# Which work stands in the turn of the loop before the first group of heads: one transformer block, two edits of the order and two extra warming products

## The chip, the cores and the metric

The kernel runs on one core of a Trainium2 chip. The metric is device time in microseconds (us), the median of three runs. The core has five engines that run side by side, each through its own list of instructions in order: TensorE (PE; its weight loads are shown apart as PEld), VectorE (DVE), ScalarE (ACT), GpSimd (POOL) and SyncE (SP, which here only issues DMA transfers). TensorE writes its results into PSUM, here eight banks of 128 x 512 float32; VectorE and ScalarE read them from there.

## The reference

The block modulates, attends and routes. With x of 8 rows x 512 tokens x 256 features and c of 8 x 256:

```
mod = (silu(c) @ wmod)                      # six vectors per row: sa, ca, ga, sb, cb, gb
h = layernorm(x) * (1 + ca) + sa
Q = h @ Wq.T ;  latent_k, latent_v = h @ Wk_down.T, h @ Wv_down.T      # 16 heads of 16, latent of 64
logits = (Q @ q_to_latent) @ latent_k.T / 8, causal
x = x + ga * (softmax(logits) @ latent_v @ v_up) @ Wout.T
h = layernorm(x) * (1 + cb) + sb
x = x + gb * (mixture of 16 experts on 512 chosen tokens each + a shared feed-forward)(h)
```

Everything is float32. Attention takes the first 570 us of the profiled execution; selection, experts and the rest of the shared feed-forward take the remainder. The change lies in the first 56 us.

## The kernel before, in words

**Set-up.** A tile `warm` of zeros is filled by VectorE, and five products of it with itself (lines 175 to 176) keep TensorE going while the inputs arrive. Each is 512 columns wide on the full 128 x 128 array; a float32 product is two instructions (two passes). Then VectorE forms the statistics of the first row's four token tiles, the first modulation `pmT` (line 207) is multiplied (16 passes of only 8 columns), VectorE takes it out of PSUM into `saT` and `caT` (lines 214 and 215), normalises the first row (`xn`), TensorE transposes it (`turn_h`, line 458), ScalarE applies the modulation, and TensorE multiplies the latents (line 468), the query (line 547) and the key (line 559) of the first group. Two row-wise modulation products per `modulate` (line 222) follow.

**Groups and turns.** The 16 heads of a row are worked on four at a time; such a group is a `Step`, n = 0 to 31, and four steps make a row. The loop runs n from -1 to 31. In turn n, the group n + 1 gets its row maxima: 16 products `scores` (line 569), each reduced by one VectorE instruction (`maxima`, line 575). At the same time the group n gets its transposed scores (`scores_t`, line 598) and ScalarE's exponentials (`exps`, line 609), after `fold` (lines 590 and 591) has turned the maxima into a column of the query, and the group n - 1 gets its products with the values (`context`, line 628). So turn -1 holds only the 16 maxima of group 0, and turn 0 holds the maxima of group 1 and the exponentials of group 0. Scores have a contraction of 32, so that each occupies a quarter of the array's rows, and their widths are 512, 384, 256 and 128 columns, four products of each.

**Query and key strips.** `query` multiplies 128 columns of Wq (two halves `c`, each two passes of 512 columns over all 128 rows); ScalarE copies the result (`spread`, line 537), and two DMAs on SP's queue (line 540) lay it out in the strips of two groups. Query and key of group 2 therefore serve groups 2 and 3 too, and are made in turn 0; group 2's scores come in turn 1.

**Order inside a turn.** `plan(n)` collects the other work of a turn as (earliest slot, estimated us, function). `laid_out` spreads it over nine slots: entries of 0.0 us go exactly where they are told; the others keep their order and are moved on, from their earliest slot, until a running budget `room` has space. `fill(k)` issues slot k: slot 0 before `fold`, slot k + 1 after the k-th pair of scores. Every engine then executes in the order in which it was issued. In turn 0 the plan holds the second modulation in transposed form (`modulate_t`, lines 225 to 240: 16 passes of 8 columns, each with its own 128 x 128 weight load, and two small VectorE instructions), four statistics of the next row, the query of group 2, its key with the first half of the values, and the second half of the values. Worked through `laid_out`, the modulation stands in slot 2, both halves of the query in slot 4, key and first values in slot 6, and the second values in slot 8.

**PSUM.** Tag "m" has two banks (`bank`), "s" and "t" three each (`bank_s`, `bank_t`). Scores of group 0 alternate between "s" and "t"; so TensorE can be six score products ahead of VectorE in turn -1, and three ahead later.

## Time and profile before

| what | value |
|---|---|
| median of three runs | 1443.43 us (1439.97 to 1443.79) |
| the profiled execution, its own time | 1438.41 us |
| its span | 1436.7 us |
| mean granted TensorE clock over the span | 0.97 |
| TensorE busy | 1379.9 us (96%) |
| VectorE busy | 906.9 us (63%) |
| start of turn 0 (first transpose of `fold`) | 31.96 us |
| start of turn 1 | 55.92 us |
| start of turn 2 | 69.53 us |

The profile divides the span into busy time per engine, a strip of 40 slices with the granted TensorE clock (`PEclk`, tenths of full speed), and groups of instructions by source line. A timeline row gives start, duration, engine, line, operation, output <- inputs, shapes and count, and in brackets the idle time of the engine before it with what ended that idle time. A table of stretches gives, for each stretch of the span, the busy time of each engine, the granted clock and the share of the DMA engines. "Busy" for TensorE means that a product is in flight, not that the array is full.

### The profile page before, as it was taken

How to read it: one execution, taken by the hardware profiler on the slowest of the kernel's cores; microseconds unless marked ns; L12 is line 12 of the kernel's file. 1: busy time of each engine (PE TensorE's matmuls, PEld its weight loads, DVE VectorE, ACT ScalarE, POOL GpSimd, SP SyncE). 2: the span in 40 equal slices, each digit the busy share in tenths (PEclk: the TensorE clock that was granted, in tenths of full speed). 3: DMA queues.
4: the chain of work that ended last, by engine and by line, in shares of the span. 5: the costliest groups of instructions: out<-in, count | busy, mean ns of one | idle time of the engine just before them, and what ended most of it. 6: DMA issues, size and time to landing. Idle time of an engine off the chain costs nothing. (4 is left out here: it accounts for less than half of the span.)

```text
span 1436.7 us, 21835 instructions
## 1 busy us (share of the span) xinstructions
PE 1379.9 (96%) x8010; PEld 932.0 (65%) x8010; DVE 906.9 (63%) x2383; ACT 475.9 (33%) x1100; POOL 561.7 (39%) x640
## 2 busy tenths in 40 slices
PE   8999999999999999997989999999999999999996
PEld 4545444444544445455555688888888888888885
DVE  4566666675666666335683477676677777776662
ACT  1455554555454553411001123232222223233221
POOL 4343524242524332402011555555444555555331
PEclk8899999999999999798999999999999999999998
DMA  7011111212121112025111434434544434434511
GB/s 235 23 28 30 46 30 41 32 41 39 49 36 41 31 42 48 22 39 206 34 35 48 128 105 134 127 86 135 137 124 116 135 102 132 133 85 130 137 16 15
DMA packets 75659, 113.28 MB, mean 79 GB/s; under 512 B 10136, under 2 KB 56856, under 8 KB 75552
## 3 DMA queue, kind: packets, MB, share of 16 engines
q1 hardware_dynamic: 60480, 85.40, 20.3%
q0 software_dynamic: 14336, 25.70, 9.3%
q8 instruction: 64, 1.05, 0.3%
q10 hardware_dynamic: 736, 0.79, 0.2%
q14 instruction: 43, 0.35, 0.1%
HBM read 86.40 MB, written 21.27 MB: 75 GB/s over the span
## 5 line engine op out<-in xcount | busy, mean ns | idle before, releaser
L575 DVE CUSTOM_DVE_ANT_0 sc_ps<-sc_ps,causal 128x256 f32<-128x256 f32 (+3 forms) x512 | 240.8, 514 | 123.2 <-PE st_ps L598 116.9
L609 ACT ACTIVATE p<-st_ps 128x256 f32<-128x256 f32 (+3 forms) x512 | 199.8, 438 | 254.9 <-PE st_ps L598 251.1
L569 PE MATMUL sc_ps<-k,q 32*128 32x512 f32 (+3 forms) x1024 | 253.1, 488 | 14.3 <-DVE mx L575 11.8
L598 PE MATMUL st_ps<-q,k 32*128 32x512 f32 (+3 forms) x1024 | 253.7, 491 | 1.5 <-ACT p L609 1.4
L613 POOL TENSOR_SCALAR_AFFINE_SELECT p<-p 128x256 f32<-128x256 f32 x256 | 104.7, 410 | 357.1 <-ACT p L609 356.4
L1114 PE MATMUL epy<-dw,emid 128*128 128x256 f32 x1024 | 236.0, 382 | 2.1 <-DVE emid L1085 1.1
L1137 POOL DMA_INDIRECT out<-eo,idx x64 | 102.6, 1602 | 318.7 <-DVE eo L1129 190.0
L1114 PEld LDWEIGHTS epy<-dw,emid 128*128 128x128 f32 x1024 | 192.0, 190 | 38.7 <-DVE emid L1085 13.2
L569 PEld LDWEIGHTS sc_ps<-k,q 32*128 32x128 f32 x1024 | 112.7, 189 | 133.4 <-DVE mx L575 80.6
L1062 ACT COPY c<-eu 128x256 f32<-128x256 f32 x120 | 44.7, 373 | 401.0 <-issue 227.5
L1045 PE MATMUL eu<-xsum,wsum 128*128 128x256 f32 x720 | 176.1, 381 | 0.0
L1045 PEld LDWEIGHTS eu<-xsum,wsum 128*128 128x128 f32 x720 | 135.7, 190 | 17.9
L1045 PE MATMUL eu<-xT,gu 128*128 128x256 f32 x480 | 142.8, 379 | 0.0
L598 PEld LDWEIGHTS st_ps<-q,k 32*128 32x128 f32 x1024 | 111.5, 190 | 7.6 <-ACT p L609 4.2
L1064 DVE TENSOR_TENSOR c<-eu,c 128x256 f32<-128x256 f32 x120 | 51.0, 425 | 100.9 <-ACT c L1063 98.5
L1085 DVE SCALAR_TENSOR_TENSOR emid<-eu,ub,esg 128x512 f32<-128x512 f32 x128 | 90.1, 743 | 30.6 <-ACT esg L1081 22.4
L1081 ACT ACTIVATE esg<-eu,gbias 128x512 f32<-128x512 f32 x128 | 81.5, 684 | 59.7 <-PE eu L1045 33.9
L1045 PEld LDWEIGHTS eu<-xT,gu 128*128 128x128 f32 x480 | 91.2, 190 | 12.4
L1065 DVE TENSOR_TENSOR eu<-eu,c 128x512 f32<-128x512 f32 x120 | 83.9, 699 | 4.1
L628 PE MATMUL po<-p,v 128*32 128x512 f32 (+3 forms) x1024 | 85.2, 452 | 0.5 <-DVE sg L297 0.4
L1002 POOL DMA_INDIRECT rows<-rows_d,idx x64 | 62.2, 972 | 40.1 <-DVE idx L995 18.4
L962 DVE TENSOR_TENSOR at_q<-pos_lo,iota 128x1024 bf16<-128x1024 f32 x64 | 75.2, 1217 | 0.0
(178 smaller groups left out, 1982.7 us busy)
## 6 DMA issues: line engine op xcount, KB each, us to landing
gu<-in_gw SPq DMA_DIRECT2D x16, 1024.0 KB, 4.9
gu<-in_up SPq DMA_DIRECT2D x16, 1024.0 KB, 7.1
dw<-in_dw SPq DMA_DIRECT2D x16, 1024.0 KB, 6.1
q<-q SPq DMA_DIRECT2D x32, 128.0 KB, 2.3
rows_d<-mod_d SPq DMA_DIRECT2D x8, 512.0 KB, 9.6
rows_d<-row SPq DMA_DIRECT2D x8, 512.0 KB, 3.0
out<-ysb SPq DMA_DIRECT2D x16, 256.0 KB, 2.1
k<-k SPq DMA_DIRECT2D x30, 128.0 KB, 2.3
```

The lines of the kernel that those rows point to most:

```text
L569: nc.tensor.matmul(sc_ps[:, 0:n], lhsT=self.q[k, i * P : (i + 1) * P], rhs=self.k[k, 0:n], start=True, stop=True)
L575: nc.vector.tensor_tensor_reduce(sc_ps[:, 0:n], sc_ps[:, 0:n], causal[:, T - n : T], 1.0, -3.0e38, ALU.add, ALU.max, self.m[:, i, o : o + 1],)
L598: nc.tensor.matmul(st_ps[:, 0:n], lhsT=self.k[k, c * P : (c + 1) * P], rhs=self.q[k, c * P : T], start=True, stop=True)
L609: nc.scalar.activation(self.p[c][:, j, :], st_ps[:, 0:n], AF.Exp, scale=SCALE)
L613: nc.gpsimd.affine_select(out=p, in_=p, pattern=[[0, 2], [1, P]], compare_op=ALU.is_ge, fill=0.0, base=0, channel_multiplier=-1,)
L628: nc.tensor.matmul(self.po[self.strip(j), c * P : T], lhsT=v[:, c, self.g * NG + j, :], rhs=self.p[c][:, j, :], start=(c == 0), stop=(c == ...
L1045: nc.tensor.matmul(self.u[:, q, :], lhsT=w, rhs=x, start=start, stop=True, skip_group_check=not start)
L1065: nc.vector.tensor_tensor(u[:, 1:3, :], u[:, 1:3, :], c3.unsqueeze(1).to_broadcast([P, 2, HC]), ALU.add)
L1081: nc.scalar.activation(sg, pg, AF.Silu, bias=gbias[:, e, f : f + 1])
L1085: nc.vector.scalar_tensor_tensor(mid[:, f, :], pu, ub[:, e, f : f + 1], sg, ALU.add, ALU.mult)
L1114: nc.tensor.matmul(self.py[:, jj, :], lhsT=self.mid[:, f, j * P : (j + 1) * P], rhs=self.dw[:, f, :], start=(n == 0), stop=(n == NF - 1),)
L1137: nc.gpsimd.indirect_dma_start(out=out[:, :], out_offset=bass.IndirectOffsetOnAxis(ap=t.idx[:, j : j + 1], axis=0), in_=eo[:, jj, :], in_o ...
```

## The change

Four edits. One more warming product of 512 columns (six in place of five) ahead of the statistics. One warming product of 256 columns after the first modulation. `modulate_t` and both halves of group 2's query leave the plan of turn 0 and enter that of turn -1, which was empty. The second half of the first row's values gets an earliest slot of 4 in place of 1 in turn 0.

Worked through `laid_out`, turn -1 then has the modulation in slot 4 (after eight of the 16 scores), the query's first half in slot 6 (after 12) and its second half in slot 8 (after all 16, ahead of `fold`). In turn 0, the key with the first values stands in slot 4, and the second values in slot 7; with an earliest slot of 1 for the latter, they would be in slot 7 as well.

```diff
-    for _ in range(5):
-        nc.tensor.matmul(bank_s("warm"), lhsT=warm[:, 0:P], rhs=warm, start=True, stop=True)
+
+    def keep_warm(n):
+        nc.tensor.matmul(bank_s("warm")[:, 0:n], lhsT=warm[:, 0:P], rhs=warm[:, 0:n], start=True, stop=True)
+
+    for _ in range(6):
+        keep_warm(T)
...
+    keep_warm(T // 2)
     nc.vector.tensor_copy(saT, pmT[:, 0:KC, :])
     nc.vector.tensor_scalar_add(caT, pmT[:, KC : 2 * KC, :], 1.0)
...
         if n < 0:
+            add(1, 1.8, modulate_t)
+            for c in range(KC):
+                add(2 + 2 * c, 0.86, lambda c=c: steps[2].query([c]))
             return todo
         if n == 0:
-            add(1, 1.8, modulate_t)
             for i in range(TT):
                 add(i, 0.0, lambda i=i: stats(TT + i, mv))
...
             for c in range(KC):
-                add(0, 0.86, lambda c=c: steps[n + 2].query([c]))
+                if n > 0:
+                    add(0, 0.86, lambda c=c: steps[n + 2].query([c]))
             if g > 0:
                 add(0, 0.9, steps[n + 2].key)
             else:
                 add(1, 1.8, lambda: (steps[n + 2].key(), rows[b].value(0)))
-                add(1, 0.9, lambda: rows[b].value(1))
+                add(1 if n > 0 else 4, 0.9, lambda: rows[b].value(1))
```

## The prediction

> **What bounds the kernel now.** I read the page first: TensorE is busy for 96% of the span, and its clock, full nearly everywhere, is lower in the first two slices.

> ```profile
> span 1436.7 us, 21835 instructions
> PE 1379.9 (96%) x8010; PEld 932.0 (65%) x8010; DVE 906.9 (63%) x2383; ACT 475.9 (33%) x1100; POOL 561.7 (39%) x640
> PEclk8899999999999999798999999999999999999998
> ```

> So I asked for the table of stretches over the first 54 us, cut where the clock changes (busy us with counts for each engine, then the clock, DMA share, GB/s).

> ```profile
> 9.26:12.67 3.41, 2.52 (x18) 2.14 (x18) 3.11 (x13) 0.00 (x0) 2.99 (x8) 1.00 1.01 345
> 12.67:16.08 3.41, 3.39 (x9) 1.95 (x9) 0.39 (x2) 1.55 (x2) 2.80 (x10) 0.50 0.02 8
> ...
> 26.32:29.74 3.42, 3.39 (x15) 1.80 (x13) 3.42 (x15) 0.00 (x0) 0.00 (x0) 1.00 1.10 350
> 29.74:33.15 3.41, 2.44 (x11) 1.74 (x9) 2.67 (x18) 0.00 (x0) 0.00 (x0) 0.50 1.11 345
> 33.15:36.56 3.41, 3.41 (x12) 1.88 (x14) 1.97 (x4) 0.54 (x2) 0.00 (x0) 0.50 1.06 371
> 36.56:39.98 3.42, 3.42 (x14) 1.81 (x9) 2.59 (x10) 1.74 (x4) 0.81 (x2) 0.50 0.07 19
> 39.98:43.39 3.41, 3.41 (x19) 3.04 (x21) 0.26 (x2) 0.00 (x0) 0.00 (x0) 0.50 0.00 0
> 43.39:46.80 3.41, 3.41 (x13) 1.34 (x8) 2.69 (x10) 1.85 (x4) 0.41 (x1) 0.50 0.00 0
> 46.80:50.22 3.42, 3.42 (x8) 1.06 (x10) 0.05 (x1) 0.28 (x1) 0.41 (x1) 0.50 0.00 0
> 50.22:53.63 3.41, 3.26 (x34) 1.96 (x30) 1.90 (x10) 2.19 (x7) 1.77 (x3) 1.00 0.36 77
> ```

> From 29.74 to 50.22 us the array runs at half clock, through nearly the whole of turn 0. The same table by turns, and the timeline around the two moved pieces:

> ```profile
> 31.96:55.92 23.96, 23.54 (x99) 13.20 (x99) 10.99 (x44) 7.97 (x20) 4.41 (x10) 0.62 0.31 93
> 55.92:69.53 13.61, 12.88 (x113) 6.91 (x113) 9.12 (x35) 7.69 (x20) 7.61 (x12) 1.00 0.02 5
> ```

> ```profile
> 38.67 3.58 PE L232 MATMUL pmT<-sc,wmod 128*128 128x8 f32 x16
> 46.13 3.78 PE L547 MATMUL pq<-hT,wq 128*128 128x512 f32 x4
> ```

> ```profile
> 42.29 0.17 DVE L239 COPY sbT<-pmT 128x16 f32<-128x16 f32 x1 [2.66 <-PE pmT L232]
> 50.74 0.43 DVE L575 CUSTOM_DVE_ANT_0 sc_ps<-sc_ps,causal 128x256 f32<-128x256 f32 x1 [3.89 <-PE st_ps L598]
> ```

> Turn 0 lasts 23.96 us, though turn 1, with more products, lasts 13.61. VectorE, busy 10.99 us of turn 0, stands idle for 2.66 and 3.89 us behind the modulation and the query: turn 0 is bound by TensorE at half clock, turn -1 (25 to 32 us) by VectorE's maxima.

> [...] TensorE counts as busy for 3.41 of 3.41 us in window after window at half clock. [...] inserted ones hold up the scores behind them, as nothing else ran from 38.67 to 42.19.

> **The change, part by part.**

> *Sixth warming product.* Two passes of 0.43: warming ends near 9.1 in place of 8.2. The modulation waits for VectorE until 9.48, so it costs nothing[...]. The *256-column product*, 0.43 us, fits between the modulation's end at 11.43 and the first transpose at 12.10. [...] Mean -0.3; bounds +0.6 and -2.

> *Turn -1.* VectorE gains the two evacuations: 42.29 to 42.55 is 0.26, so +0.3, inside its chain of maxima. TensorE has six banks of lead: scores 1 to 6 go at once, scores 7 and 8 at 25.43 and 26.08, then the modulation, 16 x 0.112 = 1.8 us at full clock (as 9.48 to 11.43), to 28.3; meanwhile VectorE needs to 29.2 for the first eight maxima, so it isn't starved. Scores 9 to 12 and the query's first half, 0.86, follow to 29.75; scores 13 to 16 wait for banks until about 30.4; the second half ends near 31.3, where `fold` waits for maxima until 32.2. At full clock all hides: +0.3. Does the clock hold? [...] At half clock the query's second half takes 1.9; TensorE's idle time before `fold`, 0.97, covers part, and what queues behind it, `fold` and with it the exponentials and turn 0's scores, is 0.9 late, and 3 to 4 when the modulation and first half are slow as well. I take +1.5 for the turn.

> *Query's copy and DMAs.* ScalarE has nothing else before the exponentials: the copy of 0.59 hides. The two issues (1.11 us) stand on SP behind the load of `shd` at 28.85 to 29.56, and find SP free. They share the DMA engines with loads until about 36.9; the strips are needed at turn 1, near 46. Nothing; if that cover went, turn 1 would start late.

> *Turn 0.* Out come 38.67 to 42.19 and 46.13 to 49.84, 3.52 + 3.71 = 7.23: 16.7 remain, still at half clock. At full clock the turn is bounded below by VectorE, 10.99 - 0.26 + about 1.1 of waiting around `fold` = 11.8, above by turn 1's 13.61. I take 13.0, and 0.5 for a half-clock beginning (fold 1.12 against 0.66): 13.5, a saving of 10.5. POOL's and ScalarE's work here, 4.41 and 7.97, stays below that. *Later values*: the same slot with either bound, so that edit itself does nothing; that the values come earlier than before is the plan's shorter total.

> Sum: -0.3 + 1.5 - 10.5 = -9.3. Afterwards nothing but the start time moves. The profiled execution would go from 1438.41 to 1429.1; it was below all three timed runs, so I set the sum against the median: 1443.43 - 9.3 = 1434.

> **Rivals.**

> *A, the forecast*: the clock is full for most of turn 0. Gains from 6 to 13: 1430 to 1437. 0.74.

> *B, the clock stays half through turn 0*: the query that used to wake it has left[...]. Then turn -1 +2.5, turn 0 at 16.7 gives -7.2, the start of turn 1 +0.7: -4, 1439.4. For it: the fall at 26 to 29 is likely; against: the same query now stands right behind it[...]. 0.17.

> *C, a transfer takes the place of the wait*: the query's strips arrive with the loads and turn 1 starts as late as before, at 56: 1443. A share of 350 GB/s for 128 KB and 10 us of margin speak against it. 0.04.

> *D, slower*: the half clock outlasts turns -1, 0 and 1. Turn -1 +4, turn 0 -7.2, turn 1, whose 12.88 us of TensorE work then takes up to 9 more: +6, 1449. It decides once turn 1 exceeds 13.6 + 3.2 = 16.8 us. [...] 0.05.

> **How the numbers follow.** About 0.3% (4.3 us) is what a measurement can tell from no change. Faster by more (below 1439.1): 0.73 of A and half of B, 0.82. Slower by more: D, 0.05. The rest 0.13. Range: A's best, no fall in turn -1 and 12.0 us for turn 0, is -13.5 with 2 us for the spread of executions (the four seen lie 5.4 apart): 1428; up to B with its neighbours: 1440.

> **What would show it.** A clock strip at full within a window or two of 34; turn 0 near 13 us, turn 1 starting at 45 to 49; no VectorE idle of 2 us in turn 0; the query's passes before `fold`; turns 1 onwards as long as before. It is wrong if the clock in turn 0 is 0.5, if `fold` starts later than 36, or if turn 1 waits for the strips.

## The result, and the profile after

| | before | changed |
|---|---|---|
| first comparison, median | 1441.70 us (4 runs) | 1422.01 us (4 runs) |
| its ratio | | 0.9873, 95% interval 0.9841 to 0.9904 |
| profiled execution, own time | 1438.41 us | 1422.49 us |
| three later comparisons, ratio | | 0.9912, 0.9915, 0.9916 (each about 0.988 to 0.995) |
| average over all executions | 1439.6 us (about 150, scatter 3.1) | 1426.2 us (29, scatter 5.0) |

The changed kernel is faster by 18.3 us in the comparison on record, and by 12 to 13.5 us when more executions are taken. The forecast was 9.3 us and a time of 1428 to 1440: the direction and the stage were right, the gain too small, and the range missed the time.

The page of the changed kernel: fewer microseconds of TensorE work in flight, and a clock strip that starts at 9 in place of 8.

```profile
span 1420.8 us, 21841 instructions
PE 1365.0 (96%) x8014; PEld 923.2 (65%) x8014; DVE 907.1 (64%) x2383; ACT 475.0 (33%) x1100; POOL 561.1 (39%) x640
PEclk9999999999999999899999999999999999999998
```

The table of stretches (busy us with counts for PE, PEld, DVE, ACT, POOL, then clock, DMA share, GB/s). The places where an execution's clock changes, counted from the kernel's start, are called its alignment below. In this one the clock falls at 28.17 us, in the trace before at 29.74.

```profile
11.11:14.52 3.41, 2.85 (x16) 1.64 (x15) 1.82 (x7) 0.72 (x2) 2.80 (x10) 1.00 0.45 143
...
24.76:28.17 3.41, 3.36 (x20) 2.45 (x20) 3.41 (x13) 0.00 (x0) 0.00 (x0) 1.00 1.08 347
28.17:31.59 3.42, 3.42 (x15) 1.26 (x18) 2.34 (x14) 0.00 (x0) 0.00 (x0) 0.50 1.10 349
31.59:35.00 3.41, 3.28 (x20) 1.51 (x24) 2.43 (x12) 0.59 (x1) 0.00 (x0) 1.00 1.08 367
35.00:38.41 3.41, 3.41 (x22) 1.65 (x14) 3.18 (x11) 2.39 (x5) 0.55 (x2) 1.00 0.63 195
38.41:41.83 3.42, 3.32 (x24) 1.73 (x24) 2.97 (x12) 2.00 (x5) 1.08 (x3) 1.00 0.00 0
41.83:45.24 3.41, 3.26 (x36) 2.33 (x28) 2.27 (x13) 2.50 (x10) 2.01 (x4) 1.00 0.37 77
```

A stretch of 3.4 us at half clock, 28.17 to 31.59, stands where there were 20.5 us, 29.74 to 50.22. The table by turns (turn 0, then turn 1), and the timeline of TensorE around the moved work:

```profile
33.14:46.15 13.01, 12.09 (x79) 6.78 (x79) 10.29 (x42) 8.22 (x22) 3.77 (x9) 1.00 0.41 125
46.15:59.70 13.55, 12.81 (x112) 6.85 (x113) 9.12 (x35) 6.99 (x18) 8.14 (x13) 1.00 0.01 2
```

```profile
26.30 1.95 PE L237 MATMUL pmT<-sc,wmod 128*128 128x8 f32 x16
28.18 1.24 PE L574 MATMUL sc_ps<-k,q 32*128 32x256 f32 x8
29.35 2.08 PE L552 MATMUL pq<-hT,wq 128*128 128x512 f32 x2
31.35 0.60 PE L574 MATMUL sc_ps<-k,q 32*128 32x128 f32 x8
31.89 1.12 PE L552 MATMUL pq<-hT,wq 128*128 128x512 f32 x2
33.14 0.66 PE L595 MATMUL pmx<-ident,mx 128*128 128x128 f32 x4
```

Turn 0 takes 13.01 us at a clock of 1.00, with VectorE busy for 10.29 of them; before it was 23.96 us at 0.62. The query's first half runs at half clock (2.08 us), its second at full clock (1.12). VectorE's timeline shows what that costs in turn -1: it waits twice for scores at half clock, first for those behind the modulation (issued at 28.18), then for those behind the query's first half (31.35).

```profile
29.43 0.43 DVE L580 CUSTOM_DVE_ANT_0 sc_ps<-sc_ps,causal 128x256 f32<-128x256 f32 x1 [0.56 <-PE sc_ps L574]
...
31.98 0.30 DVE L580 CUSTOM_DVE_ANT_0 sc_ps<-sc_ps,causal 128x128 f32<-128x128 f32 x1 [0.91 <-PE sc_ps L574]
```

**Where the rest came from.** I laid the two traces over each other, VectorE instruction by instruction. The changed kernel is 9.8 us ahead at 60 us. Then the lead changes in steps: 8.1 at 100, 9.5 at 140, 8.1 at 160, 9.5 at 240, 12.4 at 460, 10.9 at 520, 14.1 at 600, 16.3 at 780, and stays there to the end. Each step stands where one kernel's clock is at half and the other's isn't. After 60 us, until the last products, the trace before has 51.2 us at half clock, the trace after 34.1. No instruction there was touched. So two questions: is the half clock really what is paid for, and do the later 17 us belong to the change?

### The profile page after: what moved, and what is told of

Same layout as the page of the kernel before. It is cut to its first block, busy times and chain, and to the rows that moved or that the text cites. A ratio compares the mean times of both kernels' runs of the same rounds, so it can differ in the third digit from the quotient of the medians.

```text
span 1420.8 us, 21841 instructions
## 1 busy us (share of the span) xinstructions
PE 1365.0 (96%) x8014; PEld 923.2 (65%) x8014; DVE 907.1 (64%) x2383; ACT 475.0 (33%) x1100; POOL 561.1 (39%) x640
## 5 line engine op out<-in xcount | busy, mean ns | idle before, releaser
L574 PE MATMUL sc_ps<-k,q 32*128 32x512 f32 (+3 forms) x1024 | 247.8, 484 | 14.4 <-DVE mx L580 11.9
L603 PE MATMUL st_ps<-q,k 32*128 32x512 f32 (+3 forms) x1024 | 248.1, 483 | 1.4 <-ACT p L614 1.4
L574 PEld LDWEIGHTS sc_ps<-k,q 32*128 32x128 f32 x1024 | 109.3, 187 | 132.3 <-DVE mx L580 79.6
L1053 PEld LDWEIGHTS eu<-xsum,wsum 128*128 128x128 f32 x720 | 135.7, 190 | 17.9
L1093 DVE SCALAR_TENSOR_TENSOR emid<-eu,ub,esg 128x512 f32<-128x512 f32 x128 | 90.1, 743 | 28.7 <-ACT esg L1089 20.7
L1053 PEld LDWEIGHTS eu<-xT,gu 128*128 128x128 f32 x480 | 91.2, 190 | 12.4
L1010 POOL DMA_INDIRECT rows<-rows_d,idx x64 | 62.1, 971 | 38.4 <-issue 17.1
```

Source lines behind the costliest of these rows:

```text
L574: nc.tensor.matmul(sc_ps[:, 0:n], lhsT=self.q[k, i * P : (i + 1) * P], rhs=self.k[k, 0:n], start=True, stop=True)
L603: nc.tensor.matmul(st_ps[:, 0:n], lhsT=self.k[k, c * P : (c + 1) * P], rhs=self.q[k, c * P : T], start=True, stop=True)
L1053: nc.tensor.matmul(self.u[:, q, :], lhsT=w, rhs=x, start=start, stop=True, skip_group_check=not start)
L1093: nc.vector.scalar_tensor_tensor(mid[:, f, :], pu, ub[:, e, f : f + 1], sg, ALU.add, ALU.mult)
```

## The experiments

Half-clock time of an execution below is 2 x (1 - its mean granted clock) x its span; the clock's records of both traces on record hold only 1.00 and 0.50. In these traces 10.9 us of it (before) and 10.2 us (after) lie behind the last product, where no product is slowed.

**The change again, three times.** No edit.

> The changed kernel once more, to see what repeats. Both traces on record differ by 9.8 us at the start of turn 1, and by 16.2 us at the end; the 6.4 us in between come in steps of 1.4 to 3.4 us where one of the two kernels had its array clock at half and the other not. Theory CHANCE: [...] this run's falls after 60 us stand at other places than before, their total lies anywhere between 30 and 55 us, and the gain over the kernel before comes to about 10 us on the mean (ratio 0.993). Theory SYSTEM: the later gain belongs to the change; falls after 60 us total about 34 us again and the ratio is again about 0.987.

> The changed kernel again, for the size of its gain. Over the 115 timed executions so far, of five kernels, time is 1401.3 us plus 0.43 times the time at half clock, with 1.2 us of scatter; before has 90 us at half clock, the changed kernel 55 in 11 executions, the moves alone 70 in 20. Theory SUM: the changed kernel is its parts, 10 us from the moves and 1 to 2 from the warming; these executions average 1428 to 1430, and those on record were lucky alignments. Theory EXCESS: warming and moves together save more half-clock time than each by itself; the average stays at 1423 to 1426.

> The changed kernel a fourth time, for the size of its gain. 17 executions so far average 1426.1 us (scatter 5.0), 131 of before 1439.7: 13.6 us. Theory SUM: moves 9.9, warming 1.5, and the rest was alignment; the new executions average 1427 to 1430. Theory EXCESS: together they gain more than their sum; 1423 to 1426 again.

Measured: ratios 0.9912 (0.9882 to 0.9943), 0.9915 (0.9881 to 0.9948) and 0.9916 (0.9889 to 0.9943); averages 1425.5, 1428.9 and 1426.3 us in 7, 6 and 12 executions. The ratio lies between those of CHANCE (0.993) and SYSTEM (0.987); of the two later averages, one fits SUM and one lies between SUM and EXCESS. The traces start turn 1 at 48.8, 49.0 and 45.9 us and have 34.1, 47.8 and 47.8 us of later half clock. The falls aren't strewn at random, as CHANCE had it: in the first of these traces, five of the seven later falls stand where they stood in the trace on record, all 3.6 us later, as the kernel's own work there is. The first comparison's four executions (average 1423.1) were 3 us on the lucky side of the 29, and its four of before (1441.4) 2 us on the unlucky side. One of the traces shows how much the alignment does in the stage of the change itself, here the falls at 28.4 and 48.9 us with turn 0 between them:

```profile
28.40:35.20 6.80, 6.80 (x31) 4.23 (x31) 4.26 (x23) 0.00 (x0) 0.00 (x0) 0.50 1.09 356
35.93:48.80 12.87, 11.95 (x80) 6.63 (x78) 10.14 (x42) 8.31 (x22) 3.77 (x9) 1.00 0.33 87
48.90:52.30 3.40, 3.40 (x20) 1.15 (x20) 0.75 (x1) 0.00 (x0) 1.52 (x2) 0.50 0.02 5
```

Turn 0 is again 13 us; but turn -1 has 6.8 us at half clock and ends 2.7 us later, and turn 1 has 3.4.

**Before once more**, for a second trace.

> The kernel before once more, for a second trace of it. Theory CHANCE: the half-clock stretch through turn 0 is there again with 17 to 20 us, turn 1 starts at 54 to 57; the later falls stand at other places and total something other than the 51 us of the trace on record, between 30 and 60.

Measured: 1436.4 us; half clock from 28.9 us for 20.5 us, turn 0 of 23.9 us, turn 1 at 55.2 us, later half clock 47.8 us. The stretch through turn 0 isn't an accident of the trace on record. But neither are the later falls, and there CHANCE missed: each stands where it stood, 0.8 us earlier, but for one at 774 us that is gone. A third trace has the same front, that of the kernel before with unused products near its end only (below), and shows another alignment: half clock from 31.6 and from 41.9 us, for 6.8 us each, with 3.4 us at full clock between them. Turn 0 takes 21.2 us there and turn 1 starts at 54.2.

**The moves alone**, twice.

```diff
-    for _ in range(6):
+    for _ in range(5):
         keep_warm(T)
...
-    keep_warm(T // 2)
```

> The changed kernel without its two additional warming products (five of 512 columns, none of 256): only the moved modulation and query remain. Theory MOVES: turn 0 lasts about 13 us as in the changed kernel and turn 1 starts at 46 to 49; the fall of the clock around 12 us is back and costs 1 us; ratio within 0.002 of the changed kernel's. Rival WARMING: the additional warming products carry the gain beyond my forecast of 9 us; this kernel then gains 9 or less, and the changed one 17.

> The moves without the additional warming once more, beside the changed kernel: 1430.2 us on average in 20 executions. Theory SUM: 1 to 2 us above the changed kernel. Theory EXCESS: 4 us or more above it.

Measured: ratios 0.9932 (0.9912 to 0.9951) and 0.9907 (0.9872 to 0.9942); 27 executions average 1429.5 us, 10.1 below before. Turn 0 is 13.0 us in both traces, after which turn 1 starts at 48.8 and 46.5. Turn 0 of the first:

```profile
35.90:48.80 12.90, 11.98 (x80) 6.66 (x78) 10.07 (x41) 8.31 (x22) 3.83 (x9) 1.00 0.32 84
```

The moves carry most of the gain; WARMING falls.

**The warming products alone**: the kernel before with six products of 512 columns ahead of the statistics and one of 256 behind the first modulation.

> The kernel before with the two additional warming products alone. Theory MOVES: turn 0 stays at half clock and near 24 us; gain 0 to 1.5 us. Rival WARMING: gain of 5 us or more.

Measured: ratio 0.9997 (0.998 to 1.0014), average 1438.6 us in 20 executions, 1.0 us below before, which is not clear of nothing. Turn 0 is at 0.64 of the clock and takes 23.3 us. This kernel's own profiled execution took 1431.4 us, with 34.1 us of later half clock: a single trace of a kernel that gains 1 us can lie 7 below that of before. With the moves' 10.1 this makes 11.1; all 29 executions of the change gave 13.4, with a standard error of about 1. The moves' second seven executions averaged 1427.4 us, 1.1 above the twelve of the changed kernel taken beside them, as SUM has it. EXCESS isn't shown: the difference of 2.3 is within the errors of the three averages.

**Is it the clock, or that work left turn 0?** The kernel before, nothing moved, with two unused full-array products in turn -1:

```diff
+    def fill_array():
+        nc.tensor.matmul(bank("fill"), lhsT=wq[:, 0, 0:P], rhs=rows[0].hT[:, 0, :], start=True, stop=True)
+
     def plan(n):
...
         if n < 0:
+            for k in (6, 8):
+                add(k, 0.0, fill_array)
             return todo
```

> The kernel before, nothing moved, with two more products in turn -1 at the places where the changed kernel has the two halves of the query: 512 columns on all rows of the array, results unused. Theory CLOCK: they bring the clock back before or just after turn 0 starts; turn 0, which still holds modulation and query, takes 13 + 2 x 1.9 = about 16.5 us in place of 24, and the kernel gains about 7 us. Rival ORDER: what helps is that the work has left turn 0; turn 0 stays above 20 us and the kernel gains nothing.

Measured: ratio 0.9963 (0.9933 to 0.9993), average 1434.1 us in 12 executions: 5.5 below before, with 1.7 us or more of added work and nothing taken away. Turn 0 as a whole, and two of its parts, the 3.4 us at full clock that hold the modulation and the 6.8 us behind them:

```profile
35.70:55.20 19.50, 19.08 (x101) 10.06 (x100) 10.47 (x42) 7.99 (x21) 4.65 (x10) 0.82 0.25 70
```

```profile
39.20:42.60 3.40, 3.40 (x29) 2.39 (x28) 2.32 (x10) 1.21 (x3) 0.82 (x2) 1.00 0.00 0
42.60:49.40 6.80, 6.80 (x24) 2.54 (x20) 2.74 (x10) 2.40 (x5) 0.82 (x2) 0.50 0.00 0
```

The average speaks for CLOCK, and against ORDER, which expected nothing: half-clock time is 72.9 us in these executions and 88.6 in those of before, which at 0.43 us each (below) is 6.8, less the added work. The trace alone would not show it. Turn 0 is 4.4 us shorter than in the two traces of before, at a mean clock of 0.82, but it starts about 4 us later, in part behind the added products, and turn 1 starts at 55.0, only 0.2 to 0.9 us earlier. In the third alignment of the same front, without these products, turn 0 took 21.2 us and turn 1 started at 54.2. Turn 0 doesn't reach the 16.5 us that I expected: behind the modulation, still in turn 0, the clock fell again at 42.6.

**Each moved piece alone.** Query only: the modulation back in turn 0. Modulation only: the query back in turn 0, where its first half now comes in slot 0, ahead of `fold`. Both keep the additional warming.

```diff
         if n < 0:
-            add(1, 1.8, modulate_t)
             for c in range(KC):
-                add(2 + 2 * c, 0.86, lambda c=c: steps[2].query([c]))
+                add(6 + 2 * c, 0.0, lambda c=c: steps[2].query([c]))
             return todo
         if n == 0:
+            add(1, 1.8, modulate_t)
```

```diff
         if n < 0:
-            add(1, 1.8, modulate_t)
-            for c in range(KC):
-                add(2 + 2 * c, 0.86, lambda c=c: steps[2].query([c]))
+            add(4, 0.0, modulate_t)
             return todo
...
-                if n > 0:
-                    add(0, 0.86, lambda c=c: steps[n + 2].query([c]))
+                add(0, 0.86, lambda c=c: steps[n + 2].query([c]))
```

> The changed kernel with the modulation back in turn 0: only the query's two halves are in turn -1, in the same places. Theory CLOCK: a full-array product in turn -1 is what matters; turn 0 runs at full clock for most of it, with 1.9 us of modulation in it, so about 15 us; gain over the kernel before 8 to 11 us. Rival LENGTH: each moved piece gains what it took in turn 0; this one 3.7 us.

> The changed kernel with the query back in turn 0: only the modulation is in turn -1. Theory CLOCK: [...] turn 0 begins at half clock and stays there until the query's own products; turn 0 takes about 20 us, turn -1 is 0.3 to 2 us longer; gain 1.5 to 4 us. Rival LENGTH: 3.5 us from the move and more from the warming, together 5.

Measured: query only, ratio 0.9931 (0.9906 to 0.9955), average 1429.6 us, 9.7 below the average of before taken beside it (1439.3). Modulation only, 0.9972 (0.9956 to 0.9988), 1435.6 us, 3.7 below. Their turns 0, in this order:

```profile
33.20:50.10 16.90, 16.75 (x97) 10.11 (x96) 10.42 (x42) 8.12 (x21) 4.60 (x10) 0.77 0.28 83
```

```profile
35.70:53.60 17.90, 17.55 (x82) 9.95 (x81) 10.27 (x40) 8.02 (x21) 4.61 (x10) 0.62 0.27 74
```

The query, which took 3.7 us at half clock in turn 0, gains 9.7 by leaving for turn -1, about 1 of it the warming's: far more than its own length. Half-clock time is 21.5 us lower, which at 0.43 us each is 9.3. So LENGTH falls, and the gain is the clock's. (Turn 0 takes 16.9 us there, not the 15 expected; the clock fell at 40.8 us behind the modulation that stayed.) The modulation's move leaves turn 0 at a clock of 0.62, as before, with 17.9 us in place of the 20 expected; half of the query stands ahead of it here. Of its 3.7 us, lower half-clock time accounts for 1.4; where the rest comes from isn't shown. The two theories expected nearly the same of this run, so it decides little.

**Filling the hole of the modulation.** Three more unused products in turn -1 of the changed kernel.

```diff
         if n < 0:
+            for k in (2, 3, 5):
+                add(k, 0.0, lambda k=k: fill_front(k < 5))
             add(1, 1.8, modulate_t)
```

`fill_front` multiplies as `fill_array` does above, with a bank of its own for the first two, the second's bank again for the third.

> The changed kernel with three more unused full-array products in turn -1: behind scores 4 and 6, where TensorE waits for VectorE to give banks back, and behind the tenth score, after the modulation. Theory HOLE: the fall at 28 us comes from the modulation's 1.9 us of 8-column passes; with it filled the clock stays full through turn -1, fold starts at 32.3 to 32.8 in place of 33.1 to 36.1, and the kernel is 1 to 3 us below the changed one. Rival: the fillers hold up the scores, VectorE starves, fold starts later than in the changed kernel and the time is the same or 1 us more.

Measured: 0.9953 (0.9927 to 0.9979), 1433.6 us on average: 7 us slower than the changed kernel. In its trace `fold` starts at 39.5 us. HOLE falls as a way to gain, and the timeline of VectorE says why: a score stood behind the third filler, at half clock.

```profile
35.21 0.43 DVE L580 CUSTOM_DVE_ANT_0 sc_ps<-sc_ps,causal 128x256 f32<-128x256 f32 x1 [2.11 <-PE sc_ps L574]
```

The clock fell here at 32.3, for 6.8 us, so the fall had only moved from 28 to 32.

**Filling two late waits.** Nine unused products in the changed kernel, where its trace shows TensorE waiting and the clock falling: three in turn 31 and six behind the routing scores. Then the same in the kernel before, and all fillers together, with six in turn 31.

```diff
+    def fill_array(k=1):
+        for _ in range(k):
+            nc.tensor.matmul(bank_s("fill"), lhsT=shu[:, 0, 0:P], rhs=shg[:, 0, :], start=True, stop=True)
...
+        if n == len(steps) - 1:
+            for k in (3, 5, 7):
+                add(k, 0.0, fill_array)
...
+    fill_array(6)
     for i in range(TT):
         z.routed(i)
```

> The changed kernel with full-array products whose results aren't used at two places where its trace shows TensorE waiting and the clock falling in nearly each alignment: three of 512 columns in turn 31 (no maxima there), and six behind the last routing scores, where TensorE waits 5.2 us for the sigmoid. Theory CLOCK: the falls near 571, 588 and 646 us (20 us at half clock) mostly go; 0.43 x 15 = 5 to 7 us below the changed kernel, less 0.5 to 2 us that the three fillers take in turn 31. Rival: the falls there are not worth anything since VectorE and ScalarE bound these stretches; same time as the changed kernel or 1 to 2 us slower.

> The changed kernel with the nine unused products at the two late waits once more. Its four executions averaged 1420.3 us. If those were lucky alignments, 1422 to 1424 now, 3 to 5 us below the changed kernel; if not, 1420 again.

> The kernel before with the same nine unused full-array products at the two late waits as in the run of the changed kernel that had them (1420.3 us on average); nothing else. That leaves fewer late falls for chance or interaction, so the difference between the two is closer to what the change does in its own stage. Theory FRONT: the change is worth 8 to 10 us in turns -1 and 0; this kernel averages 1429 to 1431. Theory EXCESS: the change also lowers the later half-clock time in a way of its own; this kernel averages 1433 to 1435, 13 or more above the other.

> The changed kernel with both: the three products in turn -1, six in turn 31 in place of three, and six behind the last routing scores. If the gains add, 1417 to 1419 us on average. If turn 31's fillers cost more than the falls at 569 and 590 us that remained with three, 1420 to 1422.

Measured: the changed kernel with them, 0.9860 (0.9831 to 0.9890) and 0.9913 (0.9884 to 0.9942); 13 executions average 1423.7 us, 2.4 below the changed kernel, with a standard error of 1.7: the fastest average of the study, but not clear of the changed kernel's. The first four executions (1420.3) were lucky again; the next nine (1425.3) lie above the 1422 to 1424 expected. The three in turn 31 did less than expected: the fall near 570 us stayed in both traces, that near 590 in one. What the six behind the routing scores do is plain: the clock falls nowhere between 592 and 1400 us in either trace with them, where each trace of the changed kernel has a fall behind the routing scores, at 646 to 657 us. The changed kernel's trace on record, then one with the fillers:

```profile
646.00:649.00 3.00, 1.43 (x6) 1.06 (x6) 1.23 (x4) 0.58 (x1) 1.26 (x1) 0.50 0.30 51
```

```profile
640.00:652.00 12.00, 10.49 (x40) 6.47 (x39) 8.62 (x26) 0.59 (x1) 1.71 (x2) 1.00 0.50 143
```

The kernel before with them averages 1434.3 us (12 executions), 5.3 below before and 10.6 above the changed kernel with them. That was meant to tell FRONT (1429 to 1431) from EXCESS (1433 to 1435, and 13 apart); it fits neither fully. All together average 1429.5 us (18 executions), slower than the changed kernel by the front's fillers: a miss.

**What time consists of.** Over 258 executions of the six kernels without unused products, time is 1400.7 us plus 0.433 times the half-clock time, with a scatter of 1.4 us; half-clock time accounts for 95% of the variance. The same holds inside one kernel, where no instruction differs: in the 149 executions of before the factor is 0.38 and the share 91%, in the 29 of the changed kernel 0.41 and 97%. Averages:

| kernel | executions | time, us | half clock, us |
|---|---|---|---|
| before | about 150 | 1439.6 | 88.6 |
| warming only | 20 | 1438.6 | 85.8 |
| modulation only | 20 | 1435.6 | 85.3 |
| query only | 13 | 1429.6 | 67.1 |
| moves only | 27 | 1429.5 | 68.4 |
| changed | 29 | 1426.2 | 59.9 |

The change saves 28.7 us at half clock, x 0.433 = 12.4 of its 13.4 us (10.9 with the 0.38 of before alone).

## Why the prediction was wrong, step by step

*What bounds the stage*: right. Turn 0 was bound by TensorE at half clock (a mean of 0.62 over 23.96 us). The query's place decided most of it, and the modulation's the rest: with the modulation left in turn 0, the clock fell once more, at 40.8 us.

*Sixth and 256-column product, -0.3 (bounds +0.6 and -2)*: -1.0 measured alone, inside the bounds, which were my estimate, and not clear of 0. The modulation began 0.35 us later (9.83 against 9.48), and in the trace on record the fall at 12.67 was gone; in two of the three other traces of the change it was there, at 11.3 and 11.7, for 6.8 us.

*Turn -1, +1.5*: too small. `fold` starts at 33.1, 35.8, 36.1 and 32.9 us in the four traces of the change, 32.0 and 31.3 in the two of before: +2.9 on average, of which 2.4 lie between the first score and `fold` and the rest ahead of them. Whether the clock would hold there I answered with an estimate that no trace showed; it fell in all eight traces of kernels with both moves and no filler in turn -1, between 27.8 and 30.0 us, for 3.4 or 6.8 us.

*Turn 0, 13.5*: right, and the best of the steps: 13.0 in each trace. Sum of the stage: +1.18 - 10.95 = -9.8 in the trace on record, forecast -9.3. Over the four traces of the change and the two of before it is +2.9 - 11.0 = -8.1, so the close agreement of the pair on record is in part luck.

*Query's copy and DMAs, nothing*: right. SP issued them at 33.69, behind `shd`, and turn 1, at 13.55 us against 13.61 before, shows no wait for the strips.

*Later values, nothing*: right by the plan, which puts them in slot 7 with either bound; no run changes this edit alone.

*"Afterwards nothing but the start time moves"*: this step failed. I put the later stages at nothing and gave no reason. They hold 34 to 61 us of half clock in the traces of these kernels, and the two on record, with different fronts, have it at other places: the first falls after 60 us stand at 145.8 and 234.5 us before, at 89.6 and 154.5 after. In the pair on record that added 6.4 us to the gain. On average it is 13.4 less some 8 in the stage, about 5 us. Half-clock time is lower by 28.7 us on average (standard error 2.3); the traces put some 14 us of that before 60 us (23.9 in both of before; 3.4, 17.1, 17.1 and 3.4 in the four of the change). After 60 us they scatter: 34.1, 34.1, 47.8 and 47.8 us in the four traces of the change, 51.2 and 47.8 in two of before, 51.2 and 61.4 with the moves, and 34.1 with the warming alone. Yet luck alone doesn't explain the remainder. Had each execution of before lost 23.9 us early and each of the changed kernel only the 3.4 of its best traces, that would be 20.5 of the 28.7, and 8 us of half clock, or 3.5 us of time, would still have to come later, by this estimate. Why the change leads to fewer later falls stays open.

*The base and the range*: I set the sum against 1443.43, the median of three, though the profiled execution lay 5 us below it. The average of about 150 is 1439.6; from there my own sum gives 1430.3. And I allowed 2 us for the spread of executions. The changed kernel's 29 lie between 1420.3 and 1437.0; 11 of them are inside my range. From 1439.6, with the best case of 13.5 and 5 us for the scatter, its lower end would have been 1421.

*Rivals*: none of B (half clock through turn 0), C (a transfer in place of the wait) and D (slower) occurred in a trace of the change.

## What to carry to other kernels

Read the clock beside the busy share: here TensorE counted as busy for 19.5 of the 20.5 us at half clock from 29.74 to 50.22. Then ask what another place is worth to each product: the query, 3.7 us in turn 0, gained 9.7 us by leaving for turn -1, about 1 of it the warming's, and two unused full-array products there gained 5.5. Before an edit of a few microseconds is priced, see how far executions of the same kernel lie apart and why; here half-clock time accounts for 12.4 of the 13.4 us of gain and for 91% of the scatter of before, and four runs were too few. See what stands behind a filler, at half clock too: with three in turn -1, VectorE waited 2.11 us for a score behind the third, and the kernel was 7 us slower.

## What the runs showed of the hardware that I had not expected

The first rise of the clock doesn't stand still against the kernel's start: in 17 traces it lies between 4.3 and 7.7 us, and in the four of the changed kernel at 7.7, 4.5, 4.9 and 7.3. With like alignments the falls repeated: the third trace of the changed kernel and the first with the moves alone, whose first rises are 0.3 us apart, have the same eight falls between 49 and 657 us, shifted by 0.3 us.

One microsecond at half clock cost 0.43 us of time over the 258 executions of these kernels; in the profiled one of before TensorE is busy for 96% of the span.
